# A closer bound on where targets begin, BatchNorm moments joined from two parts, and a written order for the second LayerNorm's first tiles

## The chip, the cores and the metric

The kernel runs on one core of one Trainium2 chip, as one program. A core has five engines that follow their own instruction streams: TensorE (PE; its weight loads are shown apart as PEld), VectorE (DVE), ScalarE (ACT), GpSimd (POOL) and SyncE (SP), and 16 DMA engines. The metric is the device time of one execution in microseconds (us), lower is better. Three runs of the kernel before gave 1650.72, 1652.07 and 1653.43 us, so its median is 1652.07 us.

## What is computed

The reference is one layer of a graph network over 6250 nodes with 256 features and 100000 edges, whose edges come sorted by target (`dst` is sorted, and targets are drawn as 6250 u² with u uniform, so low nodes have many edges). Cut to what matters:

```
xn = layernorm(x)
neigh = segment_sum(xn[src], dst)                 # 100000 edges
h = relu(((1 + eps) * xn + neigh) @ W1 + b1) @ W2 + b2
h = (h - mean(h, 0)) * rsqrt(var(h, 0) + 1e-5) * gamma + beta      # BatchNorm over the nodes
x = x + h + mix(xn)                               # mix: linear attention and a small MLP
y = layernorm(x)                                  # the second LayerNorm
x = x + ffn(y)                                    # an LSTM along the nodes, gated prefix sums
```

## The kernel before

The nodes are cut into 125 chains of 50 steps: tile s of the second half holds node 50 c + s for every chain c (`NC`, `NS` = 125, 50). The program has five stages.

**Prologue (to about 70 us).** The edges and x are loaded, the first LayerNorm is made and `xn` is written to DRAM (`xn_d`), where the edge loop gathers from it. Edges are taken in 782 tiles of 128 and 196 groups of 4 tiles (`GT`, `GROUPS`, `GE` = 512 edges). For each group the smallest and largest target are found from `dg` (lines 206 to 214, 266 to 278), and it is checked that the targets span fewer than `W` = 96 nodes and that the smallest is not below `least(g)` (line 46), a bound worked out from the distribution of the targets. The number of groups that hold goes to `within`; if it falls short, the `If` at line 739 does the edges again by a slow path. That does not happen here.

**Edge loop (about 70 to 932 us).** The first 34 groups (`COUNTED`) are summed by another way, counting; the 162 others take one *slot* each (line 707). In a slot, POOL issues the gathers of the group two slots on, one `indirect_dma_start` per tile (line 380, tile `eg`, 10 buffers), DVE adds the sums of the slot before into the window of nodes that they belong to (`add_group`, line 411) and makes a selection matrix (`here`, line 391), and PE multiplies gathered rows with selections (line 401). Between the tiles PE does pieces of other *jobs*, which `start(slot, job)` puts on a slot. A job is a generator: each `yield` is a list of pieces for PE in that slot and at most one function after them. What follows a `yield` runs at the head of the next slot. PE, DVE and ACT issue this loop in the order in which it is written (`tc.manual_schedule`, line 703); POOL and SP are left to the scheduler.

`gin_job(b)` (line 598) is the network on block b of 125 nodes: in its first slot the first product (line 604, 8 products, recorded as 16 matmuls), in the second the ReLU (610), in the third the second product (615, again 16), in the fourth the output into `sums` (620) and the BatchNorm statistics (621, `bn_stats` into `stats[:, a, b, :]`). It may start when no later group can have a target in block b, which `first_slot(b)` (line 677) reads from `least`. The last blocks start at slots 146, 148, 150, 152, 154, 156, 158, 160, 162, 162 (b = 40 to 49). Slot 161 has the last group; slots from 162 on only finish the jobs. `mix_job(j)` (571) runs beside it, and starts for the last time at slot 155.

**BatchNorm (about 943 to 953 us).** Behind the `If` DVE aggregates all 50 blocks' statistics with one `bn_aggr` for each half of the features (line 772), makes the scale with `rsqrt` (98) and the shift (784). The scale is written into a diagonal matrix `scaled`.

**The second LayerNorm and the LSTM (about 953 to 1600 us).** `residual(s)` (865) makes tile s of the new x: PE multiplies a strided part of `sums` by `scaled` (869, into the PSUM tile `pm`, of which there are two), DVE adds `shift` (872) and `pm` (873), takes the statistics (875, 877), adds epsilon (879), POOL takes the power −1/2 (881), and DVE refines it and makes the bias (884 to 888). `normed` (893, ACT), `columns` (899, PE transposes) and `kept` (903, ACT) bring the tile into `yT`; `inputs(s)` (912) multiplies it by the input weights, 32 recorded matmuls; `step` (938) adds the recurrent product (945, 32 matmuls) and makes the gates on ACT and the state on DVE. Each chain first runs 40 warm-up steps (`WARM`), whose input products are stored and fetched again. The first three tiles are written as three `residual`, three `normed`, three `columns` and `kept`, then `inputs` and `store` of the first (lines 971 to 978); each step of the loop adds one or two more. Here no order is written: the scheduler picks, engine by engine, the earliest written instruction that it takes to be ready, so it may also run work ahead. Lines 815 to 825 (`thr`, `half`, `w_d`), for the gated sums in the loop, are written before it.

**Output (from about 1600 us).** Transposes, sums and the stores.

Of the kernel before, what the change touches and what calls it, by code (L numbers as in the profile page):

```python
# [14 lines left out]
F32 = mybir.dt.float32  # L15
I32 = mybir.dt.int32
BF16 = mybir.dt.bfloat16
AF = mybir.ActivationFunctionType
ALU = mybir.AluOpType
# [26 lines left out]
def least(g):  # L46


    return N * (g * GE / E) ** 2 - 128.0
# [27 lines left out]
def gps_layer(ctx: ExitStack, tc: tile.TileContext, x, src, dst, cols, rows, kvln, wqkv, mw1, mw2, gw1, gw2,  # L77
# [89 lines left out]
    with ExitStack() as s1:  # L167
# [3 lines left out]
        def edges_flat(t, start, ap):  # L171
            return bass.AP(tensor=t.tensor, offset=t.offset + start, ap=ap)
# [24 lines left out]
        with tc.tile_pool(name="ln1", bufs=2) as lp, tc.tile_pool(name="ps0", bufs=6, space=PSUM) as ps:  # L197
            FULL = NE // P
            tiled = []
            for name, t in (("sl", src), ("dl", dst)):  # L200
# [6 lines left out]
            real = E - (rows_g - 1) * 2 * GE  # L207
            dg = lp.tile([P, 2, GE], I32, name="dg", bufs=1)
# [4 lines left out]
            nc.scalar.dma_start(flat[rows_g - 1:rows_g, real:],  # L213
                                edges_flat(dst, E - (2 * GE - real), [[real, 1], [1, 2 * GE - real]]))
# [52 lines left out]
            for i, op in enumerate((ALU.min, ALU.max)):  # L267
# [4 lines left out]
            nc.vector.tensor_mul(place[:rows_g], place[:rows_g], place[:rows_g])  # L272
            nc.vector.tensor_scalar(place[:rows_g], place[:rows_g], least(1) - least(0), least(0), op0=ALU.mult,
                                    op1=ALU.add)
# [401 lines left out]

        def first_slot(b):
            done = [g for g in range(COUNTED - 1, GROUPS) if all(least(h) > (b + 1) * NC + 1 for h in range(g + 1, GROUPS))]
            return done[0] + 1 - COUNTED
# [18 lines left out]
        start(FOLD, fold_job())  # L698
        for j in range(NS):
            start(SUMMED + 3 + j, own_job(j))  # L700
            start(SUMMED + 5 + 1.15 * j, mix_job(j))
# [37 lines left out]
        with tc.If(held < GROUPS + PAIRS):  # L739
# [24 lines left out]
            for b in range(NS):  # L764
                for parts, _ in gin_job(b):
                    for work in parts:
                        work()


        mv = wp.tile([P, KD, 2], F32, name="bn_mv")  # L770
        for a in range(KD):
            nc.vector.bn_aggr(mv[:, a, :], stats[:, a].rearrange("p c s -> p (c s)"))
        sc = rsqrt(wp, mv[:, :, 1], [P, KD], "bn")
# [3 lines left out]
        nc.vector.tensor_add(mean, mv[:, :, 0], col("gb2", 0, KD))  # L777
# [27 lines left out]

    begin_h = wl.tile([P, KD, NC], F32, name="begin_h")
# [8 lines left out]
    nc.vector.tensor_sub(thr, col("blin", 0), col("blin", 1))  # L815

    half = wl.tile([P, 3, KD], F32, name="half")
    nc.vector.tensor_scalar(half[:, 0, :], col("fw", 0, KD), -0.5, None, op0=ALU.mult)
    nc.vector.tensor_scalar(half[:, 1, :], col("bw", 0, KD), 0.5, None, op0=ALU.mult)
    nc.vector.tensor_add(half[:, 2, :], half[:, 0, :], half[:, 1, :])  # L820
    nc.vector.tensor_scalar(half[:, 2, :], half[:, 2, :], -1.0, None, op0=ALU.mult)
    for k in range(KD):
        d = wl.tile([P, 1], F32, name="wlin_d")
        nc.vector.tensor_sub(d, col("wlin", 2 * k + 1), col("wlin", 2 * k))
        nc.vector.tensor_scalar(w_d[:, k, :], ones, d, None, op0=ALU.mult)
# [34 lines left out]
    with tc.tile_pool(name="lstm", bufs=2) as rp, tc.tile_pool(name="ps3", bufs=4, space=PSUM) as ps, \  # L860
# [4 lines left out]
        def residual(s):  # L865

            pm = ps_y.tile([P, D], F32, name="pm")
            for a in range(KD):
                nc.tensor.matmul(pm[:NC, a * P:(a + 1) * P], sums[:, a, s:s + NS * (NC - 1) + 1:NS], scaled[:, a, :],
                                 start=(a == 0), stop=True, skip_group_check=True)  # L870
            xs = xr[:NC, s, :]
            nc.vector.tensor_add(xs, xs, shift[:NC])
            nc.vector.tensor_add(xs, xs, pm[:NC])
            st = rp.tile([P, 6], F32, name="ln_st")
            nc.vector.bn_stats(st[:NC], xs)
            mv = rp.tile([P, 2], F32, name="ln_mv")
            nc.vector.bn_aggr(mv[:NC], st[:NC])
            v = rp.tile([P, 1], F32, name="ln_v")
            nc.vector.tensor_scalar(v[:NC], mv[:NC, 1:2], EPS, None, op0=ALU.add)  # L879
            r = rp.tile([P, 1], F32, name="ln_r", bufs=AHEAD)  # L880
            nc.gpsimd.tensor_tensor(r[:NC], v[:NC], minus_half[:NC], op=ALU.pow)  # L881

            t = rp.tile([P, 1], F32, name="ln_t")
            nc.vector.scalar_tensor_tensor(t[:NC], r[:NC], r[:NC], v[:NC], op0=ALU.mult, op1=ALU.mult)
            nc.vector.tensor_scalar(t[:NC], t[:NC], -0.5, 1.5, op0=ALU.mult, op1=ALU.add)
            nc.vector.tensor_mul(r[:NC], r[:NC], t[:NC])
            b = rp.tile([P, 1], F32, name="ln_b", bufs=AHEAD)
            nc.vector.scalar_tensor_tensor(b[:NC], mv[:NC, 0:1], -1.0, r[:NC], op0=ALU.mult, op1=ALU.mult)
            return s, r, b

# [77 lines left out]
        minus_half = rp.tile([P, 1], F32, name="minus_half", bufs=1)  # L968
        nc.vector.memset(minus_half, -0.5)
        fresh = iter([s for s, _ in order if s >= NS - WARM][:WARM] + list(range(NS - WARM)))  # L970
        first = [residual(next(fresh)) for _ in range(AHEAD)]
        first = [normed(*r) for r in first]
        for r in first:
            kept(*columns(*r))
        at_residual, at_columns = [], []
        h = None
        banks = inputs(order[0][0])
        store(order[0][0], banks)
# [175 lines left out]
```

## Time and profile before

| what | value |
|---|---|
| median of three runs (lowest, highest) | 1652.07 us (1650.72, 1653.43) |
| the profiled execution: device time | 1649.37 us |
| the profiled execution: span from first to last instruction | 1646.5 us |
| mean granted clock of TensorE | 0.958 |
| busy over the span: PE, PEld, DVE, ACT, POOL | 1498.1, 1398.0, 947.2, 611.7, 695.2 us |
| first gather, last gather issued | 71.49 us, 927.48 us |
| PE's last matmul of the edge loop's jobs ends | 941.88 us |
| DVE's first BatchNorm aggregation | 946.59 us |
| first input product of the LSTM | 961.24 us |

Times inside an execution are us from the start of its span. A line of the timeline gives start, duration, engine, source line, operation, what it writes and reads, how often, and in brackets how long the engine had been idle before and what released it. A line of the costliest groups gives, behind the first bar, busy time in us and the mean of one in ns; behind the second, the engine's idle time before them and what ended it. "issue" means that nothing in the profile held the instruction.

### The profile page before, as it was taken

What the parts mean: (1) busy time and instruction counts of PE and PEld (TensorE: products, weight loads), DVE (VectorE), ACT (ScalarE), POOL (GpSimd) and SP (SyncE); (2) the same over time, 40 slices, a digit from 0 to 9 for tenths busy, and PEclk for the clock granted to TensorE, in tenths of its full rate; (3) what the DMA queues carried; (4) which work ended last, traced back from release to release, by engine and by line L of the source; (5) the groups of instructions that cost most, each with busy time, mean ns of one, the idle gap of its engine ahead of it and who ended that gap; (6) DMA issues with size and microseconds to landing.
All of it is one profiled execution on the core that took longest, in us unless ns stands there. A gap on an engine that the chain in (4) does not pass through costs nothing. (4 is left out here: it accounts for less than half of the span.)

```text
span 1646.5 us, 30983 instructions
## 1 busy us (share of the span) xinstructions
PE 1498.1 (91%) x11312; PEld 1398.0 (85%) x11312; DVE 947.2 (58%) x3028; ACT 611.7 (37%) x1866; POOL 695.2 (42%) x713
## 2 busy tenths in 40 slices
PE   1688899899989969999999889999999999999985
PEld 1477788888889969998999879999999998888864
DVE  6878778888842212222222285555555556777777
ACT  2553323433311114333332244555554434444440
POOL 0277777777777747777777400000000000000005
PEclk9689989999989979999999989999999999999996
DMA  9533333333346683333333321111111001333214
GB/s 243 188 89 98 102 101 100 100 100 99 101 142 177 172 196 103 104 106 105 104 106 105 117 74 65 54 60 64 63 64 64 26 1 63 96 94 88 88 51 157
DMA packets 57708, 166.00 MB, mean 101 GB/s; under 512 B 13040, under 2 KB 21879, under 8 KB 55669
## 3 DMA queue, kind: packets, MB, share of 16 engines
q0 software_dynamic: 31008, 84.71, 18.2%
q1 hardware_dynamic: 22884, 75.07, 14.2%
q10 hardware_dynamic: 3652, 4.11, 1.1%
q8 instruction: 93, 1.52, 0.4%
q14 instruction: 71, 0.58, 0.1%
HBM read 130.56 MB, written 33.28 MB: 100 GB/s over the span
## 5 line engine op out<-in xcount | busy, mean ns | idle before, releaser
L380 POOL DMA_INDIRECT eg<-xn_d,si x646 | 643.5, 996 | 220.3 <-issue 99.0
L401 PE MATMUL pg<-here,eg 128*128 128x96 f32 x2584 | 399.5, 281 | 54.7 <-DMA eg<-xn_d,si 40.5
L401 PEld LDWEIGHTS pg<-here,eg 128*128 128x128 f32 x2584 | 363.9, 198 | 86.3 <-DMA eg<-xn_d,si 43.3
L954 ACT ACTIVATE gate<-pg,b_l 128x125 f32<-128x125 f32 x718 | 201.8, 366 | 229.7 <-PE pg L945 228.4
L411 DVE TENSOR_TENSOR sums<-sums,pg 128x192 f32 x162 | 57.4, 354 | 381.9 <-PE pg L401 200.5
L912 PE MATMUL pg<-yT,w_ih 128*128 128x125 f32 x1600 | 186.9, 275 | 0.0
L945 PE MATMUL pg<-sums,w_hh 128*128 128x125 f32 x1568 | 183.1, 275 | 0.0
L912 PEld LDWEIGHTS pg<-yT,w_ih 128*128 128x128 f32 x1600 | 182.7, 192 | 0.1
L945 PEld LDWEIGHTS pg<-sums,w_hh 128*128 128x128 f32 x1568 | 179.0, 192 | 0.0
L881 POOL TENSOR_TENSOR ln_r<-ln_v,minus_half 125x1 f32<-125x1 f32 x50 | 27.4, 552 | 343.1 <-DVE ln_v L879 314.5
L1083 POOL TENSOR_TENSOR xr<-xr,rest_t 125x1024 f32<-125x1024 f32 x8 | 22.9, 2898 | 312.3 <-DVEq L1028 312.3
L945 PE MATMUL pg<-h_w,w_hh 128*128 128x125 f32 x1248 | 146.0, 276 | 0.2 <-ACT x_out L920 0.2
L945 PEld LDWEIGHTS pg<-h_w,w_hh 128*128 128x128 f32 x1248 | 143.1, 192 | 0.6 <-ACT x_out L920 0.4
L620 ACT ACTIVATE sums<-mm,vec 128x125 f32<-128x125 f32 x100 | 36.5, 365 | 269.5 <-DVE sums L411 178.8
L604 PE MATMUL mm<-sums,g 128*128 128x125 f32 x800 | 119.1, 285 | 1.8 <-DVE counts L643 1.6
L615 PE MATMUL mm<-z,g 128*128 128x125 f32 x800 | 114.7, 284 | 1.0 <-ACT z L610 1.0
L604 PEld LDWEIGHTS mm<-sums,g 128*128 128x128 f32 x800 | 106.6, 198 | 5.3 <-issue 1.8
L455 PE MATMUL mm<-m,xnT 128*125 128x256 f32 x400 | 107.9, 394 | 0.6 <-DVE counts L643 0.5
L615 PEld LDWEIGHTS mm<-z,g 128*128 128x128 f32 x800 | 102.0, 196 | 1.1 <-ACT z L610 1.1
L463 ACT ACTIVATE mm<-kv 125x512 f32<-125x512 f32 x50 | 30.1, 602 | 190.7 <-DVE kv L460 190.7
L610 ACT ACTIVATE z<-mm,vec 128x125 f32<-128x125 f32 x200 | 56.3, 367 | 91.5 <-PE mm L604 91.5
L391 DVE TENSOR_TENSOR here<-iota,drel 128x384 f32<-128x384 f32 x162 | 89.3, 551 | 0.0
(239 smaller groups left out, 2162.6 us busy)
## 6 DMA issues: line engine op xcount, KB each, us to landing
x_d<-x_out SPq DMA_DIRECT2D x40, 500.0 KB
x_in<-x_d SPq DMA_DIRECT2D x40, 500.0 KB
xr<-in_x_dram SPq DMA_DIRECT2D x10, 1120.0 KB
eg<-xn_d,si POOLq DMA_INDIRECT x646, 2.8
counts<-xn_d SPq DMA_DIRECT2D x16, 384.0 KB
xn_d<-xn SPq DMA_DIRECT2D x5, 1120.0 KB
out_dram<-o SPq DMA_DIRECT2D x12, 448.0 KB
xr<-in_x_dram SPq DMA_DIRECT2D x10, 130.0 KB
```

Of the source, the lines that this page charges most:

```text
L380: nc.gpsimd.indirect_dma_start(out=g, out_offset=None, in_=xn_d[:], in_offset=bass.IndirectOffsetOnAxis(ap=at, axis=0))
L391: nc.vector.tensor_tensor(here[:, :n, :], iota[:, None, :W].to_broadcast([P, n, W]), drel[:, gi * GT:gi * GT + n, None].to_broadcast([P, n ...
L401: nc.tensor.matmul(pg[:, k, :], g[:, k * P:(k + 1) * P], here[:, i, :], start=(i == 0 and k == 0), stop=(i == n - 1), skip_group_check=True)
L411: nc.vector.tensor_add(window, window, pg)
L455: nc.tensor.matmul(pkv[:r, at], xnT[:, k, j * NC:(j + 1) * NC], w_qkv[:, k, D:][:, at], start=(k == 0 and half == 0), stop=(k == KD - 1), ...
L604: nc.tensor.matmul(p1[:, m, :], g1[:, k, m * P:(m + 1) * P], sums[:, k, at], start=(m == 0 and k == 0), stop=(k == KD - 1), skip_group_che ...
L610: nc.scalar.activation(z1[:, m, :], p1[:, m, :], AF.Relu, bias=col("gb1", m))
L615: nc.tensor.matmul(p2[:, a, :], g2[:, m, a * P:(a + 1) * P], z1[:, m, :], start=(a == 0 and m == 0), stop=(m == 2 * KD - 1), skip_group_ch ...
L620: nc.scalar.activation(sums[:, a, at], p2[:, a, :], AF.Identity, bias=col("gb2", a))
L912: nc.tensor.matmul(pg[:, SLOT[g], :], w_ih[:, k, block(g, a)], yT[:, k, s * NC:(s + 1) * NC], start=(i == 0 and k == 0), stop=False, skip_ ...
L945: nc.tensor.matmul(banks[a][:, SLOT[g], :], w_hh[:, k, block(g, a)], h[:, k, :], start=False, stop=(k == KD - 1), skip_group_check=True)
L954: nc.scalar.activation(gate[g], pg[:, SLOT[g], :], AF.Tanh if g == G else AF.Sigmoid, bias=bias(g, a))
```

## The change

Three parts, and what hangs on them.

1. `least(g)` becomes N u² − 257 (u³ (1 − u))^½ − 10 with u = g·512/100000, in place of N u² − 128. The same bound is worked out on the chip for the check: in the prologue DVE has 7 small operations and ACT one in place of 2 on DVE. The end of the last row of `dg` is filled by three small DMAs in place of one, all on ACT's queue. Most `gin_job`s start one slot earlier; the last ones as listed below.
2. The BatchNorm moments of blocks 0 to 45 are aggregated by a new job that runs at the end of slot 159, those of blocks 46 to 49 behind the `If`, and five small operations of DVE join the two.
3. The first three tiles of the second LayerNorm get a written order on PE, DVE and ACT: the statistics of two tiles, then the first tile up to its input products, then the second and the third. A written order holds only among the instructions inside it; others may still fall between them. `residual` is cut in two (`moved`, `scales`), and in every tile `pm` is now added before `shift`. Lines 815 to 825 move to the end of that order; `minus_half` is set by POOL, earlier.

First slots of `gin_job` by the two bounds:

```
b         38  39  40  41  42  43  44  45  46  47  48  49
before   141 143 146 148 150 152 154 156 158 160 162 162
after    140 143 145 147 149 151 153 155 157 159 160 162
```

The diff, cut to its core:

```diff
 def least(g):
-    return N * (g * GE / E) ** 2 - 128.0
+    u = g * GE / E
+    return N * u * u - SLACK * (u ** 3 * (1 - u)) ** 0.5 - 10.0
+SLACK = 6.5 * 2 * N / E ** 0.5
...
+            last = E - (GROUPS - 1) * GE
...
-            nc.scalar.dma_start(flat[rows_g - 1:rows_g, real:],
-                                edges_flat(dst, E - (2 * GE - real), [[real, 1], [1, 2 * GE - real]]))
+            for at in range(real, 2 * GE, last):
+                n = min(last, 2 * GE - at)
+                nc.scalar.dma_start(flat[rows_g - 1:rows_g, at:at + n], edges_flat(dst, E - n, [[real, 1], [1, n]]))
...
-            nc.vector.tensor_mul(place[:rows_g], place[:rows_g], place[:rows_g])
-            nc.vector.tensor_scalar(place[:rows_g], place[:rows_g], least(1) - least(0), least(0), op0=ALU.mult,
-                                    op1=ALU.add)
+            nc.vector.tensor_scalar(place[:rows_g], place[:rows_g], GE / E, None, op0=ALU.mult)
+            square = lp.tile([P, 2], F32, name="square", bufs=1)
+            nc.vector.tensor_mul(square[:rows_g], place[:rows_g], place[:rows_g])
+            cube = lp.tile([P, 2], F32, name="cube", bufs=1)
+            nc.vector.tensor_mul(cube[:rows_g], square[:rows_g], place[:rows_g])
+            nc.vector.tensor_scalar(place[:rows_g], place[:rows_g], -1.0, 1.0, op0=ALU.mult, op1=ALU.add)
+            nc.vector.tensor_mul(cube[:rows_g], cube[:rows_g], place[:rows_g])
+            nc.scalar.activation(cube[:rows_g], cube[:rows_g], AF.Sqrt, scale=SLACK * SLACK)
+            nc.vector.tensor_scalar(place[:rows_g], square[:rows_g], float(N), -9.0, op0=ALU.mult, op1=ALU.add)
+            nc.vector.tensor_sub(place[:rows_g], place[:rows_g], cube[:rows_g])
...
+        LATE = 4
+        bn_mv = [wp.tile([P, KD, 2], F32, name=f"bn_mv{i}") for i in range(2)]
+        def moments(i):
+            of = slice(0, NS - LATE) if i == 0 else slice(NS - LATE, NS)
+            for a in range(KD):
+                nc.vector.bn_aggr(bn_mv[i][:, a, :], stats[:, a, of].rearrange("p c s -> p (c s)"))
+        def early_job():
+            yield [], partial(moments, 0)
...
+        start(max(first_slot(NS - LATE - 1), first_slot(0)) + 4, early_job())
...
-            nc.vector.bn_aggr(mv[:, a, :], stats[:, a].rearrange("p c s -> p (c s)"))
-        sc = rsqrt(wp, mv[:, :, 1], [P, KD], "bn")
+        late = LATE / NS
+        moments(1)
+        (m0, v0), (m1, v1) = ((mv[:, :, 0], mv[:, :, 1]) for mv in bn_mv)
+        apart = wp.tile([P, KD], F32, name="apart")
+        nc.vector.tensor_sub(apart, m1, m0)
+        nc.vector.scalar_tensor_tensor(v0, v1, late / (1 - late), v0, op0=ALU.mult, op1=ALU.add)
+        nc.vector.scalar_tensor_tensor(m0, apart, late, m0, op0=ALU.mult, op1=ALU.add)
+        nc.vector.tensor_mul(apart, apart, apart)
+        nc.vector.scalar_tensor_tensor(v0, apart, late, v0, op0=ALU.mult, op1=ALU.add)
+        sc = rsqrt(wp, v0, [P, KD], "bn", scale=1 - late)
...
-        def residual(s):
+        def moved(s):
...
+            nc.vector.tensor_add(xs, xs, pm[:NC])
             nc.vector.tensor_add(xs, xs, shift[:NC])
-            nc.vector.tensor_add(xs, xs, pm[:NC])
...
+            return s, mv, v
+        def scales(s, mv, v):
...
+        def residual(s):
+            return scales(*moved(s))
...
-        first = [residual(next(fresh)) for _ in range(AHEAD)]
-        first = [normed(*r) for r in first]
-        for r in first:
-            kept(*columns(*r))
+        with tc.manual_schedule(engines={mybir.EngineType.PE, mybir.EngineType.DVE, mybir.EngineType.Activation}):
+            first = moved(next(fresh))
+            second = moved(next(fresh))
+            kept(*columns(*normed(*scales(*first))))
+            banks = inputs(order[0][0])
+            kept(*columns(*normed(*scales(*second))))
+            kept(*columns(*normed(*residual(next(fresh)))))
...
+            nc.vector.tensor_sub(thr, col("blin", 0), col("blin", 1))
...
+        store(order[0][0], banks)
...
-        banks = inputs(order[0][0])
-        store(order[0][0], banks)
```

More of the change, by code (lines that the diff above doesn't have):

```diff
@@ L767, in gps_layer @@
                         work()
-        mv = wp.tile([P, KD, 2], F32, name="bn_mv")
-        for a in range(KD):
-            nc.vector.bn_aggr(mv[:, a, :], stats[:, a].rearrange("p c s -> p (c s)"))
-        sc = rsqrt(wp, mv[:, :, 1], [P, KD], "bn")
+            moments(0)
+        late = LATE / NS
[8 more added lines that the diff above has]
+        sc = rsqrt(wp, v0, [P, KD], "bn", scale=1 - late)
         nc.vector.tensor_mul(sc, sc, col("gamma", 0, KD))
         mean = wp.tile([P, KD], F32, name="bn_mean")
-        nc.vector.tensor_add(mean, mv[:, :, 0], col("gb2", 0, KD))
+        nc.vector.tensor_add(mean, m0, col("gb2", 0, KD))
         nc.vector.scalar_tensor_tensor(mean, mean, -1.0, sc, op0=ALU.mult, op1=ALU.mult)
@@ L804, in bias @@
         return b_l[:, g * KD + a:g * KD + a + 1]
+    minus_half = wl.tile([P, 1], F32, name="minus_half")
+    nc.gpsimd.memset(minus_half, -0.5)
     begin_h = wl.tile([P, KD, NC], F32, name="begin_h")
@@ L814, in gps_layer @@
     thr = wl.tile([P, 1], F32, name="thr")
-    nc.vector.tensor_sub(thr, col("blin", 0), col("blin", 1))
     half = wl.tile([P, 3, KD], F32, name="half")
[L818 to L825, printed above, removed]
     one_r = ones[:, :NC]
@@ L967, in gps_layer @@
         order = [(s, True) for s in range(NS - WARM, NS)] + [(s, False) for s in range(NS)]
-        minus_half = rp.tile([P, 1], F32, name="minus_half", bufs=1)
-        nc.vector.memset(minus_half, -0.5)
         fresh = iter([s for s, _ in order if s >= NS - WARM][:WARM] + list(range(NS - WARM)))
-        first = [residual(next(fresh)) for _ in range(AHEAD)]
-        first = [normed(*r) for r in first]
-        for r in first:
-            kept(*columns(*r))
+        h = None
+        with tc.manual_schedule(engines={mybir.EngineType.PE, mybir.EngineType.DVE, mybir.EngineType.Activation}):
[6 more added lines that the diff above has]
+            nc.vector.tensor_sub(thr, col("blin", 0), col("blin", 1))
+            nc.vector.tensor_scalar(half[:, 0, :], col("fw", 0, KD), -0.5, None, op0=ALU.mult)
+            nc.vector.tensor_scalar(half[:, 1, :], col("bw", 0, KD), 0.5, None, op0=ALU.mult)
+            nc.vector.tensor_add(half[:, 2, :], half[:, 0, :], half[:, 1, :])
+            nc.vector.tensor_scalar(half[:, 2, :], half[:, 2, :], -1.0, None, op0=ALU.mult)
+            for k in range(KD):
+                d = wl.tile([P, 1], F32, name="wlin_d")
+                nc.vector.tensor_sub(d, col("wlin", 2 * k + 1), col("wlin", 2 * k))
+                nc.vector.tensor_scalar(w_d[:, k, :], ones, d, None, op0=ALU.mult)
+        store(order[0][0], banks)
         at_residual, at_columns = [], []
-        h = None
-        banks = inputs(order[0][0])
-        store(order[0][0], banks)
         fetched = {}
```

## The prediction, made before the changed kernel had run

> **What bounds the kernel now.** I read the costliest groups first, then busy time by stretch, then the timeline around each place that the change touches.
>
> ```profile
> L380 POOL DMA_INDIRECT eg<-xn_d,si x646 | 643.5, 996 | 220.3 <-issue 99.0
> 820.00:870.00 50.00, 49.28 (x410) 48.09 (x409) 12.97 (x36) 16.15 (x50) 37.82 (x41) 1.00 0.37 105
> 1110.00:1310.00 200.00, 200.00 (x1695) 200.00 (x1695) 113.51 (x433) 99.44 (x316) 14.66 (x27) 1.00 0.14 58
> ```
>
> (Stretches: length, then busy us of PE, PEld, DVE, ACT, POOL; clock; DMA.) POOL issues a gather every 0.95 + 0.30 = 1.25 us from 71.49 to 927.48 (but for a stall at 580 to 612, while x is loaded again), whatever PE does. PE is nearly full too: between 611 and 929 it waits for gathers 7 times, 5.5 us in all, the last two times at 772.31 (0.81) and 929.15 (0.79). In the LSTM PE is hardly ever idle. So the edge loop ends with PE's backlog behind POOL's last gather, the LSTM's length is PE's work, and what lies between is a chain of latencies. Anything gained there goes to the end one for one; the output stage is untouched.
>
> The end of the edge loop, and BatchNorm (timeline):
>
> ```profile
> 927.48 0.95 POOL L380 DMA_INDIRECT eg<-xn_d,si  x1 [0.30 <-issue]
> 929.15 0.69 PE L401 MATMUL pg<-here,eg 128*128 128x96 f32 x4 [0.79 <-DMA eg<-xn_d,si]
> ...
> 932.58 2.14 PE L615 MATMUL mm<-z,g 128*128 128x125 f32 x16 [0.96 <-ACT z L610]
> ...
> 934.56 3.74 PE L604 MATMUL mm<-sums,g 128*128 128x125 f32 x32
> ...
> 938.14 3.74 PE L615 MATMUL mm<-z,g 128*128 128x125 f32 x32
> ...
> 943.03 0.29 DVE L621 BATCH_NORM_STATS2 stats<-mm 128x6 f32<-128x125 f32 x1 [0.43 <-ACT sums L620]
> ...
> 946.59 2.88 DVE L772 BATCH_NORM_AGGREGATE bn_mv<-stats 128x2 f32<-128x300 f32 x2 [3.26 <-DVEq L739]
> 949.50 0.17 DVE L101 TENSOR_SCALAR bn_v<-bn_mv 128x2 f32<-128x2 f32 x1
> ```
>
> Behind the last gather PE still has five half jobs of 16 matmuls (1.87 us each), then statistics, the branch, and 2.88 us of aggregation alone. The second LayerNorm's start:
>
> ```profile
> 955.42 3.14 PE L869 MATMUL pm<-stats,sums 128*125 128x128 f32 x12 [1.08 <-DVE xr L873]
> ...
> 957.04 0.56 POOL L881 TENSOR_TENSOR ln_r<-ln_v,minus_half 125x1 f32<-125x1 f32 x1 [28.61 <-DVE ln_mv L877]
> ...
> 959.45 0.60 ACT L893 ACTIVATE y<-xr,ln_b,ln_r 125x256 f32<-125x256 f32 x1 [9.54 <-DVE ln_t L885]
> ...
> 961.24 1.81 PE L912 MATMUL pg<-yT,w_ih 128*128 128x125 f32 x14
> ...
> 963.56 0.43 PE L899 MATMUL pt<-ident,y 125*128 125x125 f32 x2 [0.51 <-ACT y L893]
> ...
> 971.15 3.84 PE L945 MATMUL pg<-h_w,w_hh 128*128 128x125 f32 x32 [0.23 <-ACT x_out L920]
> ```
>
> The reader should see that the first tile's chain takes 6.4 us from `shift` (ready at 953.08) to y, and that PE used its waiting to run six tiles' L869 ahead.
>
> **Part 1, earlier blocks.** No product is added; most blocks start one slot earlier, so at each wait for a gather PE has on average one half job (1.87 us) less ahead of it. From the wait at 929.15 the old end, 941.88, loses: one half job, 1.87; the 0.96 for the ReLU of block 47, since block 48's second product now fills that place; and gains about 0.5, for block 49's ReLU (0.37 on ACT and handing over) has nothing beside it. That is −2.3. From 772.31 the later waits go as well: −1.87 − 0.79 − 0.96 + 0.5 = −3.1. The later end holds: −2.3, less 0.2 for DVE in slot 159 (below): **−2.1**. Bounds: −1.0 if PE, now fuller, meets new waits on DVE's sums; −3.7 if a whole job leaves the tail. POOL doesn't move: it runs up to ten tiles ahead and PE held it up for under 3 us in the whole loop.
>
> The prologue pays. DVE is busy almost without a break from 13.77 to 56.7 and leads to the last xn, its store and the first gather. Five more small DVE operations, at some 0.08 from start to start (as L270 and L271 there), are +0.4; the new root on ACT fits before its first root at 26.11. Two more small DMAs stand on ACT's queue ahead of the weights (L219 at 12.58, L221 at 13.10) and before ACT's table load at 22.72; 2.1 us lie between its end (24.0) and ACT's first use (26.11), which covers them. DVE's first wait in line is the `dg` load:
>
> ```profile
> 13.77 1.21 DVE L283 TENSOR_REDUCE pairs<-dg 17x4 f32<-17x1024 int32 x1 [2.80 <-DMA dg<-in_dst_dram]
> ```
>
> It reads 17 rows, all from the first piece, issued at 4.14 and not moved, so I take no delay. If it waits for the last piece, which moves from 10.54 to the place that L221 has now, 13.10, it costs 2.6. **+0.4**, between 0 and +3.0.
>
> **Part 2, the moments.** Of the 2.88 us behind the branch, two aggregations over 24 numbers remain. The rows give 1479 ns for 300 numbers and 178 for 6 (L877), so 4.4 ns a number, about 260 ns for 24; two take some 0.45. The joining adds five operations, four of them in a chain at 0.20 from start to start (as L105 to L109): 0.85. 2.88 becomes 1.3: **−1.55** (−1.3 to −1.7). ACT's table load ends at 947.2, before the root needs it. [...]
>
> The early half, 2 × 1.48 × 46/50 = 2.7 us, goes to DVE in slot 159. PE's work there is four tiles (2.15) and two half jobs (3.74), 5.9 us; DVE has 0.35 + 0.55 else. Behind it stand the next add (L411), ACT's output of a block and PE's next first product; they need DVE about when it ends, so I count 0.2; without that cover 2.7. [...] The trace shows such a case: the gather at 79.22 takes 6.84 us instead of 0.95, beside L362's 6.08. If the aggregation did so, POOL's last gathers would slip by up to 2.7. But [...] the gathers beside L391 or L621 keep to 0.95; I take nothing.
>
> **Part 3, the written order.** Lines 815 to 825 no longer stand before the first tile. `pm` is ready at about 953.4; the five operations to `v` take 1.7 (at 993.27 the same chain without `shift` takes 1.43 to POOL). POOL's power runs beside the second tile's five, which end at 956.7; four more at 0.2, and y starts at 957.6 instead of 959.45: −1.85. The transposes and the copy follow as before (1.79), so L912 starts at 959.4. The waits of 0.51 and 0.23 go: −0.7. Against it: what PE no longer does while waiting. With two `pm` tiles and the third tile placed behind the second's transposes, I count four tiles' L869 done by then or in gaps, not six: 2 × 0.84 (four matmuls between 992.10 and 992.94), one pair of transposes 0.25, and 0.35 waiting for the second copy: +2.3. **−0.25**, from −1.9 (six run ahead all the same) to +1.5 (only the two written first, and a wait before L945). `pm` before `shift` adds nothing: same operations, and DVE is half idle there.
>
> Sum: −2.1 + 0.4 − 1.55 − 0.25 = −3.5. The profiled execution's 1649.37 (span 1646.5) becomes 1645.9; it lies 2.7 below the median of the runs, which becomes 1652.07 − 3.5 = **1648.6**. Differences under 0.2% (3.3 us) are about what a measurement here can't tell from none.
>
> **Rivals.** *More than counted:* PE's backlog shrinks by the bound from 772.31 (−3.1) and the scheduler fills PE's waits with L869 (−1.9): −3.1 + 0.4 − 1.55 − 1.9 = −6.2, 1645.9. For it: PE idles some 4 us from 952 to 961. Against: only two `pm` tiles. *It doesn't do what it says:* blocks start earlier but PE meets new waits (−1.0), and the LayerNorm gives back 1.5: −1.0 + 0.4 − 1.55 + 1.5 = −0.7, 1651.4. For it: PE at 98% in 820 to 870. *Slower:* the third tile's L869, statistics, power and transposes form a chain of 1.9 + 0.8 + 0.9 + 0.8 = 4.4 us on one written PE order. If the scheduler puts the second tile's L912 behind those transposes, PE stands still from 964.3 for about 4.2: +0.7, 1652.8. It decides whether L912 of tile two starts before the third's L899. Against: the written order doesn't bind L912 of tile two.
>
> **Chances.** Forecast 0.50 (own range 1647.2 to 1650.0; 0.30 of it below 1648.77), more 0.20, nothing 0.18, slower 0.12 (0.07 of it, with `dg` or the scheduler's other choices on top, above 1655.4). Faster 0.50, same 0.43, slower 0.07. Range 1645.4 to 1652.6.
>
> **What would show it.** Right: the last L615 ends 2 us earlier after the last gather; 1.3 us from the first aggregation behind the branch to the first operation of `rsqrt`; the first L912 some 6.3 us behind `shift`, PE full after it. Wrong: gathers starting later than 72; a gather over 2 us near slot 159; a PE gap of 4 us near 964.

## The result and the profile after

The kernel after takes 1647.73 us in the median of 10 runs (1644.14 to 1650.74); the kernel before took 1651.53 us beside it (10 runs). The ratio is 0.9974, with a 95% interval of 0.9964 to 0.9984: 2.6 to 5.9 us less. The prediction of 1648.6 us holds. Its steps hold less well: the edge loop's end and the moments are near, and the written order, forecast as a small gain, is a loss.

The profiled execution of after took 1648.64 us, its span is 1646.9 us, 0.4 *longer* than the span of before. Single executions differ by some 4 us either way, so the two profiles are compared stage by stage and the stages' sum is left to the medians. Line numbers are those of the kernel after, unless a line is said to be another's: gathers L395, their products L416, the network's products L619 and L630, aggregations L698, `shift` L819, `pm` L896, transposes L933, input products L946, recurrent products L979.

The end of the edge loop in the timeline of after:

```profile
922.83 2.65 DVE L698 BATCH_NORM_AGGREGATE bn_mv<-stats 128x2 f32<-128x276 f32 x2
...
927.78 0.95 POOL L395 DMA_INDIRECT eg<-xn_d,si  x1 [0.30 <-issue]
...
932.93 0.59 PE L416 MATMUL pg<-here,eg 128*128 128x96 f32 x4
933.35 2.87 PE L630 MATMUL mm<-z,g 128*128 128x125 f32 x24
936.05 1.95 PE L619 MATMUL mm<-sums,g 128*128 128x125 f32 x16
938.52 2.14 PE L630 MATMUL mm<-z,g 128*128 128x125 f32 x16 [0.52 <-ACT z L625]
```

The jobs end at 940.66, 12.88 us behind the last gather's issue; before it was 941.88 and 14.40. Behind the last L416 stand three and a half half jobs instead of five. The early aggregation lies beside three gathers, which keep to 0.95 to 0.97 us, so it did not hold POOL up. PE also catches up with the gathers less often. Its longest waits from 620 to 942 us, before and then after (total us, times, longest):

```profile
PE pg L401 <- DMA eg<-xn_d,si: 5.5, 7, 1.8
PE mm L587 <- DVE stats L621: 2.9, 5, 0.6
PE mm L576 <- DVE stats L621: 1.8, 3, 0.6
```

```profile
PE mm L602 <- DVE stats L636: 4.1, 7, 0.6
PE mm L591 <- DVE stats L636: 2.3, 4, 0.6
PE pg L416 <- DMA eg<-xn_d,si: 2.2, 4, 1.3
```

Waiting for gathers falls by 3.3 us, waiting for DVE's statistics rises by 1.7. With the experiments below that ran at about 1650 us there are three profiles with the old bound and seven with the new one. Over this stretch, the waits for statistics are 4.7 to 4.8 us in the three and 6.4 to 6.6 in the seven, those for gathers, less evenly, 4.4 to 5.5 and 1.4 to 4.5. BatchNorm and the start of the LSTM, in the timeline of after:

```profile
945.52 0.39 DVE L698 BATCH_NORM_AGGREGATE bn_mv<-stats 128x2 f32<-128x24 f32 x2 [3.40 <-DVEq L767]
...
946.72 0.17 DVE L106 TENSOR_SCALAR bn_v<-bn_mv 128x2 f32<-128x2 f32 x1
...
949.71 1.92 PE L896 MATMUL pm<-stats,sums 128*125 128x128 f32 x8
955.73 0.68 PE L933 MATMUL pt<-ident,y 125*128 125x125 f32 x2 [4.09 <-DVE ln_b L919]
956.86 5.50 PE L946 MATMUL pg<-yT,w_ih 128*128 128x125 f32 x32 [0.46 <-ACT yT L937]
...
962.41 1.46 PE L896 MATMUL pm<-stats,sums 128*125 128x128 f32 x6
963.71 3.73 PE L946 MATMUL pg<-yT,w_ih 128*128 128x125 f32 x32
967.63 0.43 PE L933 MATMUL pt<-ident,y 125*128 125x125 f32 x2 [0.19 <-ACT y L927]
967.90 0.59 PE L896 MATMUL pm<-stats,sums 128*125 128x128 f32 x2
968.33 3.73 PE L979 MATMUL pg<-h_w,w_hh 128*128 128x125 f32 x32
```

From the first aggregation behind the branch to the root's first operation it is now 1.20 us (2.91 before). Then the two lines of L946: the same 32 matmuls take 5.50 us the first time and 3.73 the second. PE has stood still for 4.09 us just ahead of the first. The granted clock, by stretch, in after (the figure behind the busy times):

```profile
944.00:960.00 16.00, 6.79 (x28) 6.14 (x29) 7.70 (x39) 2.95 (x5) 1.22 (x3) 0.50 0.01 4
960.00:962.00 2.00, 2.00 (x18) 2.00 (x18) 0.00 (x0) 1.37 (x2) 0.00 (x0) 0.91 0.00 0
```

and in before:

```profile
960.00:962.00 2.00, 2.00 (x15) 1.94 (x16) 1.56 (x10) 1.27 (x4) 0.66 (x2) 1.00 0.00 0
```

In this execution of before, PE ran other tiles' `pm` products in its wait, and its clock was full at 960, ahead of the first input product at 961.24. After, PE idled, and most of that product ran at half clock. Other executions of the old order, below, had the half clock there too, so these two profiles alone don't show that the run-ahead keeps the clock. To compare the LSTM's start fairly I take the time from `shift` (L784; L819) to the first matmul that takes a stored input, L933 before and L967 after: by then the same work has been done. In before, and then in after:

```profile
1368.39 1.85 PE L933 MATMUL pg<-x_in,ident 128*128 128x500 f32 x4
```

```profile
949.96 0.42 DVE L819 TENSOR_TENSOR shift<-shift,mm 128x256 f32<-128x256 f32 x1 [1.06 <-PE mm L817]
...
1368.33 1.84 PE L967 MATMUL pg<-x_in,ident 128*128 128x500 f32 x4
```

`shift` starts at 952.66 before, so before takes 415.73 us and after 418.37. The written order *costs* 2.6 us here. The profiled spans add up: end of the jobs −1.22, to the aggregation +0.15, to the root −1.71, to `shift` +0.08, to the stored input +2.64, the rest +0.46, together +0.40.

### The profile page after: what moved, and what is told of

Its sections match the earlier page's. It is cut to its first block, busy times and chain, and to the rows that moved or that the text cites. A ratio compares the mean times of both kernels' runs of the same rounds, so it can differ in the third digit from the quotient of the medians.

```text
span 1646.9 us, 31001 instructions
## 1 busy us (share of the span) xinstructions
PE 1504.0 (91%) x11312; PEld 1401.6 (85%) x11312; DVE 953.7 (58%) x3039; ACT 615.1 (37%) x1867; POOL 693.0 (42%) x714
## 5 line engine op out<-in xcount | busy, mean ns | idle before, releaser
L395 POOL DMA_INDIRECT eg<-xn_d,si x646 | 641.4, 993 | 222.5 <-issue 96.0
L416 PE MATMUL pg<-here,eg 128*128 128x96 f32 x2584 | 398.8, 280 | 50.4 <-DMA eg<-xn_d,si 43.7
L416 PEld LDWEIGHTS pg<-here,eg 128*128 128x128 f32 x2584 | 361.9, 198 | 83.8 <-DMA eg<-xn_d,si 48.0
L946 PE MATMUL pg<-yT,w_ih 128*128 128x125 f32 x1600 | 188.6, 276 | 0.5 <-ACT yT L937 0.5
L946 PEld LDWEIGHTS pg<-yT,w_ih 128*128 128x128 f32 x1600 | 184.3, 193 | 0.9 <-ACT yT L937 0.9
L979 PE MATMUL pg<-sums,w_hh 128*128 128x125 f32 x1568 | 183.1, 275 | 0.0
L979 PEld LDWEIGHTS pg<-sums,w_hh 128*128 128x128 f32 x1568 | 179.0, 192 | 0.0
L979 PE MATMUL pg<-h_w,w_hh 128*128 128x125 f32 x1248 | 145.6, 275 | 0.0
L979 PEld LDWEIGHTS pg<-h_w,w_hh 128*128 128x128 f32 x1248 | 143.0, 192 | 0.0
L619 PE MATMUL mm<-sums,g 128*128 128x125 f32 x800 | 117.9, 282 | 0.3 <-DVE sums L426 0.2
L630 PE MATMUL mm<-z,g 128*128 128x125 f32 x800 | 116.1, 286 | 0.5 <-ACT z L625 0.5
L619 PEld LDWEIGHTS mm<-sums,g 128*128 128x128 f32 x800 | 105.4, 195 | 3.6 <-issue 0.8
L630 PEld LDWEIGHTS mm<-z,g 128*128 128x128 f32 x800 | 103.5, 199 | 0.7 <-ACT z L625 0.7
```

What stands on the lines that cost most here:

```text
L395: nc.gpsimd.indirect_dma_start(out=g, out_offset=None, in_=xn_d[:], in_offset=bass.IndirectOffsetOnAxis(ap=at, axis=0))
L416: nc.tensor.matmul(pg[:, k, :], g[:, k * P:(k + 1) * P], here[:, i, :], start=(i == 0 and k == 0), stop=(i == n - 1), skip_group_check=True)
L619: nc.tensor.matmul(p1[:, m, :], g1[:, k, m * P:(m + 1) * P], sums[:, k, at], start=(m == 0 and k == 0), stop=(k == KD - 1), skip_group_che ...
L630: nc.tensor.matmul(p2[:, a, :], g2[:, m, a * P:(a + 1) * P], z1[:, m, :], start=(a == 0 and m == 0), stop=(m == 2 * KD - 1), skip_group_ch ...
L946: nc.tensor.matmul(pg[:, SLOT[g], :], w_ih[:, k, block(g, a)], yT[:, k, s * NC:(s + 1) * NC], start=(i == 0 and k == 0), stop=False, skip_ ...
L979: nc.tensor.matmul(banks[a][:, SLOT[g], :], w_hh[:, k, block(g, a)], h[:, k, :], start=False, stop=(k == KD - 1), skip_group_check=True)
```

## The experiments

Each run is measured beside the kernel before on its own chip. On two of these chips the kernel before takes 1650.3 to 1650.5 us; on two others, where the run with PE left to the scheduler and the halves of the slots took place, it takes about 1775.

**Which part gains?** Theory A: the gain lies in the edge loop's tail and in the moments, and the written order adds nothing or costs, because PE idles and meets its first product at half clock. Theory B: the written order carries the gain. Part 1 alone (the new bound, its check and the `dg` loads):

```diff
 def least(g):
-    return N * (g * GE / E) ** 2 - 128.0
+    u = g * GE / E
+    return N * u * u - SLACK * (u ** 3 * (1 - u)) ** 0.5 - 10.0
...
+            nc.scalar.activation(cube[:rows_g], cube[:rows_g], AF.Sqrt, scale=SLACK * SLACK)
```

> The kernel before with the closer bound alone (block starts, the check on the chip, the three small loads). Theory A (the gain lies in the edge loop's tail and in the moments, the written order adds nothing): PE's last product of the jobs ends 1 to 2 us earlier, so -1.2 us or so against before, 0 to -2.2. Theory B (the gain of the medians lies in the written order, the earlier blocks only move PE's waits): within 0.5 us of before, and the last product ends where it did relative to the last gather.

Measured: 1646.29 us (before beside it 1650.5), ratio 0.9973 [0.9960, 0.9986]. That is more than either theory had. In its trace PE waits for a gather for the last time here:

```profile
790.50 0.66 PE L416 MATMUL pg<-here,eg 128*128 128x96 f32 x4 [0.16 <-DMA eg<-xn_d,si]
```

From 790.50 to the end of the jobs it is PE's own work, with its short waits for DVE and ACT, that sets the time in this execution, no longer POOL's. Part 3 alone (the written order and what moves with it):

```diff
-        first = [residual(next(fresh)) for _ in range(AHEAD)]
...
+        with tc.manual_schedule(engines={mybir.EngineType.PE, mybir.EngineType.DVE, mybir.EngineType.Activation}):
+            first = moved(next(fresh))
...
```

> The kernel before with the written order of the second LayerNorm's first tiles alone. Theory A: the first input product starts about 1.7 us sooner behind shift, but PE then stands idle before it, so its clock is still 0.5 for about 3.4 us of that product (32 matmuls in about 5.3 us in place of 3.65) and the tiles run ahead are fewer; the later steps lie 2 to 2.6 us later behind shift than before; time +1.5 to +2.6. Theory B: the profile of after was one unlucky phase of the clock; the order is worth -1 to -2.

Measured: 1653.17 us, ratio 1.0017 [1.0010, 1.0025]: a loss of 1.7 to 4.1 us. Its trace repeats the pause and the slow product:

```profile
959.41 0.68 PE L898 MATMUL pt<-ident,y 125*128 125x125 f32 x2 [4.10 <-DVE ln_b L884]
960.54 5.44 PE L911 MATMUL pg<-yT,w_ih 128*128 128x125 f32 x32 [0.46 <-ACT yT L902]
```

From `shift` to the stored input it takes 418.33 us. Parts 1 and 2, which is the kernel after with the old lines of part 3:

```diff
-        with tc.manual_schedule(engines={mybir.EngineType.PE, mybir.EngineType.DVE, mybir.EngineType.Activation}):
-            first = moved(next(fresh))
...
+        first = [residual(next(fresh)) for _ in range(AHEAD)]
...
```

> The changed kernel without the written order: the closer bound and the joined moments, with the second LayerNorm as before. Theory A: faster than the changed kernel by 1.5 to 2.6 us, -4 to -6 against before, if the medians of after hold as they are; at least -2.7 (shift came 2.70 us earlier in the profile). Theory B: slower than the changed kernel by 1 to 2 us, -2 to -3 against before.

Measured: 1643.11 us, ratio 0.9956 [0.9939, 0.9972], and 415.73 us from `shift` to the stored input. Theory B has fallen: the written order alone loses time, and without it the kernel gains 7.3 us against before (4.6 to 10.1), where theory A had 4 to 6. That it beats the kernel after as well is seen in the stage, 415.73 us against 418.37; the intervals of the two ratios still overlap a little. Part 2 alone:

```diff
+        start(max(first_slot(NS - LATE - 1), first_slot(0)) + 4, early_job())
...
-            nc.vector.bn_aggr(mv[:, a, :], stats[:, a].rearrange("p c s -> p (c s)"))
+        moments(1)
...
```

> Part 2 alone: the old bound, no written order, but the moments joined from blocks 0 to 45 and 46 to 49; by the old bound the early aggregation falls into slot 160. Counting theory: 1.2 us instead of 2.91 from the first aggregation behind the branch to the first operation of rsqrt, the wait for the last products as before (14.4 us from the last gather to the end of the jobs), so -1.7 us: about 1648.8 where before gives 1650.5. Rival, the early aggregation of 2.65 us delays PE in the last full slot: end of the jobs 15 to 17 us behind the last gather, and no gain.

Measured: 1649.49 us, ratio 0.9996 [0.9985, 1.0007]. The medians can't tell 1.7 us from nothing. Its trace shows the stage: 945.42 to 946.63 from the aggregation to the root, 1.21 us, and the jobs end 14.10 us behind the last gather, as in before, so the early aggregation held nothing up.

**What does the written order cost?** First try: 22 identity products on PE behind the branch and 16 behind the second tile's `pm` (results unused), to bring the clock up.

```diff
+        for _ in range(22):
+            nc.tensor.matmul(idle[:, :P], ident, ident, start=True, stop=True)
         late = LATE / NS
...
             second = moved(next(fresh))
+            for _ in range(16):
+                nc.tensor.matmul(idle[:, 0, :], ident, ident[:, :NC], start=True, stop=True)
```

> The changed kernel with 22 products of the identity with itself on PE behind the branch and 16 more behind the second tile's pm, whose results nobody reads: nothing is left out, work is added where PE stood idle. Theory A (the half clock is what the written order costs): granted clock 1.0 at the first input product, its 32 matmuls in 3.7 in place of 5.3 us, BatchNorm's small products and pm sooner by 0.5 to 1 us; -1.7 to -2.7 against the changed kernel. Theory B (PE's clock does not matter, the lost run-ahead does): 0, or +0.5 where the added products stand in the way.

Measured: 1648.89 us, ratio 0.9989 [0.9981, 0.9997], not better than after. L801 and L1013 are the fillers, L949 the input product:

```profile
944.95 7.15 PE L801 MATMUL mm<-ident 128*128 128x128 f32 x43 [0.74 <-issue]
951.94 0.61 PE L820 MATMUL mm<-ident,bn_mean 128*128 128x128 f32 x4
...
959.25 3.84 PE L949 MATMUL pg<-yT,w_ih 128*128 128x125 f32 x32 [0.46 <-ACT yT L940]
```

The input product did run at full clock, 3.84 us, and from `shift` (952.59) to the stored input (1369.06) it takes 416.47 us, 1.90 less than in after. But the first filler took 7.15 us, some 60% of it at half clock (0.50 until 949.4), and held `shift` up: L820 came at 951.94, where after has it 3.1 us behind the aggregation, which would be 946.7. The filler was too long, and the total doesn't show what the clock is worth. The second try keeps only a short filler, in the pause itself:

```diff
             second = moved(next(fresh))
+            for _ in range(12):
+                nc.tensor.matmul(idle[:, 0, :], ident, ident[:, :NC], start=True, stop=True)
```

> The kernel after with 12 identity products on PE (results unused) between the second tile's pm and the first transposes. Theory A, the half clock costs: PE then has no pause of 4 us ahead of the first input product, which takes 3.8 us instead of 5.5; from shift to the first fetched-input matmul 416.5 instead of 418.4; about 1646, 1.8 us less than after. Rival B, only the lost run-ahead of pm products costs: 418.4 and 1647.7 as after.

```profile
951.50 3.53 PE L1010 MATMUL pg<-ident 128*128 128x125 f32 x24
956.70 3.84 PE L946 MATMUL pg<-yT,w_ih 128*128 128x125 f32 x32 [0.46 <-ACT yT L937]
```

Measured: 1645.56 us, ratio 0.9964 [0.9950, 0.9978], and 416.48 us from `shift` to the stored input, 1.89 less than after. In this stage, products that compute nothing make the kernel faster; the ratios of the whole, 0.9964 and 0.9974, are too near to tell. So in the written order the half clock costs 1.9 us of the 2.6, as two executions with it (418.37, 418.33) and two without (416.47, 416.48) agree; the other 0.75 remains.

**Did the old order keep the clock?** I took it from the profile of before that PE's run-ahead brings the clock back in time. The other traces, put side by side, say that it need not. "First input products" are the matmuls up to the first other instruction of PE:

| run | order on PE | first input products | from `shift` to the stored input |
|---|---|---|---|
| before, part1_only | left to the scheduler | 14 in 1.81 us | 415.73, 415.75 us |
| parts12 | left to the scheduler | 14 in 2.60 us | 415.73 us |
| slots_only | left to the scheduler | 14 in 2.81 us | 415.80 us |
| part2_only | left to the scheduler | 14 in 3.19 us | 416.25 us |
| after, part3_only | written | 32 in 5.50 and 5.44 us | 418.37, 418.33 us |
| warm, fill | written, with filler | 32 in 3.84 us | 416.47, 416.48 us |

In three of the five executions of the old order the clock was 0.50 when the first input product began. Yet the stage took no more than 0.5 us longer. In parts12 (its L947 is the input product, L934 the transposes, L980 the recurrent product):

```profile
957.51 2.60 PE L947 MATMUL pg<-yT,w_ih 128*128 128x125 f32 x14
959.95 0.38 PE L934 MATMUL pt<-ident,y 125*128 125x125 f32 x2
...
967.09 3.77 PE L980 MATMUL pg<-h_w,w_hh 128*128 128x125 f32 x32
```

The third tile's transposes and the first recurrent product start without a wait, where PE waited 0.51 and 0.23 us ahead of them in before. So the slow product seems to fill waits that PE would have had; no run tests this alone. What the old order has in every execution is the work done early, six tiles' `pm` ahead of the first input products, against two in after.

**Can the early start be had without the idling?** Parts 1 and 2 with lines 815 to 825 written behind the first tiles, and nothing else of part 3:

```diff
-    nc.vector.tensor_sub(thr, col("blin", 0), col("blin", 1))
...
         for r in first:
             kept(*columns(*r))
+        nc.vector.tensor_sub(thr, col("blin", 0), col("blin", 1))
...
```

> Parts 1 and 2 without the written order, and lines 815 to 825 (thr, half, w_d) written behind the first tiles as in the kernel after, otherwise scheduled freely. Theory A, the start of the written order comes from these ten DVE operations being out of the way, and run-ahead products keep the clock: y 5.1 to 5.8 us behind shift instead of 6.8, shift to the first fetched-input matmul 414.7 instead of 415.7, about 1 us under parts 1 and 2 alone. Rival, PE's waits are set by the second and third tile's chains: no change against parts 1 and 2.

Measured: 1644.3 us, ratio 0.9965 [0.9950, 0.9981], so not under parts 1 and 2 (0.9956). y does come earlier, 5.64 us behind `shift` instead of 6.79, but the stored input comes 416.18 us behind it instead of 415.73. L893 is `pm` here, L923 the transposes:

```profile
950.97 2.98 PE L893 MATMUL pm<-stats,sums 128*125 128x128 f32 x12 [0.24 <-DVE xr L897]
...
956.45 0.43 PE L923 MATMUL pt<-ident,y 125*128 125x125 f32 x2 [0.67 <-ACT y L917]
```

Five tiles' `pm` are done ahead here, six in parts 1 and 2, and PE waits 0.67 for the second y. That fits the rival of this run, that the second and third tile set PE's waits. It is not shown: the clock fell to 0.50 again from 957.6 to 961.1, in the middle of the input products, which costs time as well. In the last form DVE and ACT keep the written order and PE is left to the scheduler:

```diff
-        with tc.manual_schedule(engines={mybir.EngineType.PE, mybir.EngineType.DVE, mybir.EngineType.Activation}):
+        with tc.manual_schedule(engines={mybir.EngineType.DVE, mybir.EngineType.Activation}):
```

> The kernel after with the written order on DVE and ACT only; PE is left to the scheduler, which puts seven tiles' pm products (14 instead of 4 instructions) ahead of the first transposes. Theory A, run-ahead products keep the clock and are work that is needed anyhow: first input product at full clock, y 5.1 us behind shift, from shift to the first fetched-input matmul 414 to 416 instead of 418.4; 1643.5 to 1645. Rival B, pm has two buffers and DVE's written order frees them late, so that the products queue in front of the transposes and hold the first tile up: 418 or more, 1647.7 or worse.

This run fell on a third chip, where the kernel before takes 1775.29 us, so only ratios are compared. Measured: 0.9960 [0.9944, 0.9976].

```profile
1078.60 5.20 PE L946 MATMUL pg<-yT,w_ih 128*128 128x125 f32 x32
```

y comes 7.10 us behind `shift` (1068.91), not 5.1: DVE takes the `pm` of two more tiles, at 1073.06 and 1074.70, before the first tile's bias is done. The first input product runs mostly at half clock, 0.50 until 1081.5. So theory A's total came true (0.9960 is what its 1643.5 to 1645 us would be of 1650), its y and its clock did not. The stored input still comes at 416.16, against 415.98 and 416.41 in two kernels there that have no written order (the two halves of the slots, below). With PE's run-ahead both the early start and the loss are gone, and the clock was not the reason: the run-ahead is worth its time even where the half clock stays.

**Where in part 1?** Part 1 gave 4.5 us by its ratio (2.3 to 6.6), where the prediction has 1.7 (2.1 less 0.4). The new slots alone, with the check and the loads of before:

```diff
 def least(g):
-    return N * (g * GE / E) ** 2 - 128.0
+    u = g * GE / E
+    return N * u * u - SLACK * (u ** 3 * (1 - u)) ** 0.5 - 10.0
...
-            nc.vector.tensor_scalar(place[:rows_g], place[:rows_g], least(1) - least(0), least(0), op0=ALU.mult,
+            nc.vector.tensor_scalar(place[:rows_g], place[:rows_g], N * (GE / E) ** 2, -128.0, op0=ALU.mult,
```

> Only the new bound for the slots; the check on the chip keeps the old, wider bound and the dg load of before (the check is then weaker than the schedule relies on, the computation is the same). Part 1 gave 4.2 us, I had predicted 1.7. Theory S, the surplus lies in the slots: -4 to -4.6, 1646.2, with the end of the jobs 12.4 us behind the last gather and the last gather a microsecond or two earlier than before. Rival P, the surplus is chance of single executions or lies in the prologue: -2.0, 1648.5.

Measured: 1647.02 us, ratio 0.9975 [0.9966, 0.9985]; the prologue's share is not to be seen beside 0.9973. The total is theory S's. Its signs in the trace are not: the jobs end 13.22 us behind the last gather, not 12.4, and the last gather is issued at 929.22, not earlier than before. Then the slots of blocks 40 to 49 alone, and those of the others alone:

```diff
-            done = [g for g in range(COUNTED - 1, GROUPS) if all(least(h) > (b + 1) * NC + 1 for h in range(g + 1, GROUPS))]
+            low = least if b >= 40 else least_wide
+            done = [g for g in range(COUNTED - 1, GROUPS) if all(low(h) > (b + 1) * NC + 1 for h in range(g + 1, GROUPS))]
```

> As the run with the new bound for the slots alone, but only blocks 40 to 49 take their slots from it; blocks 0 to 39 keep those of before. The question is where the 4 us of the slots (1647.02 against 1650.34) lie, of which the profiled executions show 1.6 behind the last gather (12.7 us on average instead of 14.25). Theory T, all of it is the tail: the same gain, near 1646.5, with the end of the jobs 12.7 us behind the last gather. Rival L, 1.6 is the tail and the rest comes in the loop, from the slots of the early blocks: about 1648.5 here.

> The other half: only blocks 0 to 39 take their slots from the new bound, blocks 40 to 49 keep those of before. Theory T (all of the gain is the tail): 1650.3, no change, the end of the jobs 14.3 us behind the last gather. Rival L (2.5 us come from the loop): about 1648, with POOL waiting 2 to 3 us less between 86 us and the last gather.

> The new slots for blocks 40 to 49 alone once more: the first time it ran where the edge loop lasted 975 us instead of 856, PE waited for gathers 7 us instead of 39 and none of the two halves of the slots gained anything. If before runs near 1650 here: theory T, all of the slots' 4 us is the tail, 1646.5; rival L, 1.6 is the tail (end of the jobs 12.7 us behind the last gather instead of 14.25) and the rest comes from the early blocks or is chance, 1648.5. Where PE's waits for gathers are few again: no change from before.

The first gave 0.9996 [0.9983, 1.0010] on the third chip and, once more, 0.9991 [0.9979, 1.0003] on a fourth, where the kernel before takes 1774.99 us; the second, which has `b < 40` in the condition, 1.0004 [0.9991, 1.0016] on the third. Neither half gains anything that can be seen there. The edge loop lasts some 975 us on these chips instead of 856, PE's mean granted clock in it is 0.92 to 0.93 instead of 0.97, and PE seldom catches up with the gathers: it waits 6.9 to 11.6 us for them in the loop, where the kernel before at 1650 us waits 39.4. What slows these chips down is not settled.

Two readings of this are not safe. That the new slots gain by waits for gathers is one: over the whole loop these waits are 39.4 to 43.6 us with the old bound and 38.6 to 45.3 with the new one, in the ten executions at 1650 us. They fall behind 620 us only, by some 2.4 us on average. That the new slots gain nothing on the slow chips is the other: the form with PE left to the scheduler has all of them, and gained 7.1 us (4.3 to 9.9) on the third chip. Part 2 can account for 1.7 of it, and the LSTM's start for next to nothing. The slots as a whole were not run alone there.

## Why the prediction was right, step by step

**Part 1, the tail** (−2.1, bounds −1.0 and −3.7). The mechanism is right, the size near: over the executions profiled on chips where before takes about 1650 us, the jobs end 14.25 us behind the last gather with the old bound (three of them: 14.40, 14.26, 14.10) and 12.69 with the new one (seven, 12.24 to 13.22): −1.6. A likely reason for its being smaller is the one of the lower bound, in another form: PE, now fuller, waits more for DVE, though for its statistics and not for its sums, +1.7 us. No run tests this alone. I had taken the wait at 929.15 as the place from which the loss is counted. In part 1 alone no wait for a gather is left behind 790.50, so there the end is not counted from a gather at all; the slots alone, with the same starts, have one of 0.89 us as late as 925.40.

**Part 1, the prologue** (+0.4). The first reduction of `dg` starts at 13.73 (13.77 before), so the load did not wait for the small pieces, as I took it. On ACT's queue they pushed the table load from 22.72 to 25.21 and used up the 2.11 us of cover; the first root came at 26.51 instead of 26.11. That these 0.4 us equal my number is luck: I had counted them on DVE and called the queue covered. The first gather came at 74.62, past my sign of 72. That is no effect of the change: in part 3 alone, with the prologue of before, it comes at 74.90. It costs little, since the gathers then stand still beside DVE's 6.08 us at 80; the first one behind that comes at 86.45 (86.36 before).

**Part 1, in the medians.** They give more than the profiles show: −4.1 [−5.6, −2.5] for the slots alone, while the profiled executions end their jobs at 941.77 on average with the old bound and at 940.16 with the new one, also −1.6. Three and seven executions that differ by over 2 us among themselves can't settle where the other 2 us lie, and the runs meant to tell fell on slower chips. Why the new slots give more than their tail stays open. So the total came out right partly by luck: a surplus in part 1 that I can't explain offset a loss in part 3 that I had not seen.

**Part 2** (−1.55). 2.91 became 1.20, −1.71: the two aggregations over 24 numbers took 0.39 instead of my 0.45, the joining 0.81 instead of 0.85. The 2.65 us of the early half (I had 2.7) lay beside three gathers. The 0.2 us that I counted for it in slot 159 are not seen: PE's next first product does start 0.61 us behind the start of the product ahead of it, where 0.43 is usual, but it does so in part 1 alone too, which has no early half.

**Part 3** (−0.25, bounds −1.9 and +1.5). This step failed: +2.6, beyond its upper bound. Two of its terms did. The first is the lost run-ahead. I had counted four tiles' `pm` as done by the start of the first input product "or in gaps", instead of six. Only two were (the 8 records at 949.71), and the next two came at 962.41 and 967.90, where PE had no gap. The second has no term at all: I took the first input product at its full speed, and 32 matmuls in 5.50 instead of 3.73 are +1.8.

The sum can be done again up to the first recurrent product. The first input product starts 1.68 us sooner behind `shift` (I had 1.85), and waits of 0.51 and 0.23 shrink to one of 0.19. Against this stand 1.8 for the clock, two tiles' `pm` (8 × 0.21 = 1.7) and a pair of transposes (0.25) that now fall into this stretch, less 12 matmuls of the third tile's input product (12 × 0.117 = 1.4) that no longer do: −1.68 − 0.55 + 1.8 + 1.7 + 0.25 − 1.4 = +0.1, where −0.1 is measured (18.37 us behind `shift` instead of 18.49). By then the kernel after has done two tiles' `pm` and those 12 matmuls less than before, 1.7 + 1.4 = 3.1 us of work. That makes 3.0, against 2.6 measured; the rest is not accounted for.

The two terms are not independent. With the filler the clock's share goes and 0.75 us remains. With the old order the half clock comes in some executions too and costs at most 0.5. So the loss is the early work given up, together with a first input product at half clock for which PE had no more waits to hide it in. That the profile of before showed this product at full clock was chance.

**The rivals.** "More than counted" wanted −1.9 from part 3 and falls there. "It doesn't do what it says" had the LayerNorm giving back 1.5; the give-back was larger, but part 1 and part 2 did more than it allowed. The slower one did not happen: L946 of tile two starts at 963.71, ahead of the third tile's L933 at 967.63, and PE has no gap of 4 us near 964. The gap of 4.09 us was ahead of the first tile's transposes, where I did not look for it.

## What to carry to other kernels

Before writing an order by hand for a chain of latencies, see what the engine does in its waits now: work that it will need later is worth its time, even at half clock (415.73 us from `shift` to the stored input in parts12, whose first input product began at half clock, against 418.37 in after). PE's first products behind the wait of 4.1 us ran mostly at half clock here (32 in 5.50 us in after and 5.44 in part3_only, instead of 3.73), although the trace of before, in the old order, shows the first ones at full clock (14 in 1.81 us). Cost them so, and ask which waits behind them could take up the delay. And judge a step by its own stage, with more than one execution: here the total was right while one step had the wrong sign and another gave, in the medians, over twice its number.

## What the runs showed of the hardware

PE's clock falls and rises with its own work here. In after it fell from 1.00 to 0.50 at 943.3, 2.6 us behind the last product's end at 940.66, and rose again at 960.4, 3.5 us after PE had begun to work without a pause at 956.86. In before it fell at 945.1, 3.2 us behind the last product's end at 941.88; in the run with the short filler it was still 1.00 at 946.0, 5.0 us behind the end at 940.96. There PE is busy almost from 948.67 on, the clock rises at 952.9 (0.72 on average from 946 to 958, 1.00 from 956 on), and it is still full at the first input product, at 956.70.

How long the clock stayed at 0.50 can be read in rows of 0.1 us: from 945.10 to 958.75 in before (13.65 us), from 943.30 to 960.37 in after (17.07) and from 942.28 to 959.34 in parts12 (17.06). In these three traces that is four, five and five times 3.41 us; nothing here shows what sets this step. In before the clock was back 6.1 us behind `shift`, in parts12 10.8, with the same order on PE. So one and the same order meets its first input product at either clock.

The first input product of after spends 3.5 us at half clock, from 956.86 to 960.4, and so loses half of that, 1.75 us (an estimate from this trace); 1.8 is measured (5.50 us against 3.73). With this term my step of −0.25 would have come out as a loss.

A fact that the sum rested on held as well: DVE's aggregation, 2.65 us long beside the gathers, left them at 0.95 to 0.97 us, where beside its scalar multiplication of 6.08 us one of them takes nearly as long (6.16 us in after, from 79.99 on; 6.84 in before).
